# A macaron block on one core: the first phase's tile steps, queued behind the main stream's latest product and lookup

## The chip, the core and the metric

The kernel runs on one core of a Trainium2 chip. The metric is the device time of one execution in microseconds, the median over runs on the chip. The kernel before has 1830.85 us, the median of three runs (1830.73 to 1833.56).

## The reference

The input x has 2 x 2048 tokens of 256 features, 4096 tokens in all. Three residual steps follow one another:

```python
x = x + 0.5 * ffn(layernorm(x), router_w, rg, ru, rd, sg, su, sd)
x = x + attn(layernorm(x), w_qkv, ln_w, w_proj)
x = x + 0.5 * ffn(layernorm(x), router_w, rg, ru, rd, sg, su, sd)
```

The feed-forward part has a shared branch and a routed one. The shared branch sends every token through a gated pair of 256 x 2048 matrices and back: `silu(x @ sg) * (x @ su) @ sd`. The routed branch computes 8 logits of each token, takes the best two experts with weights that add to one, gathers up to 640 tokens for each expert in their order, runs the same kind of gated network with 1024 hidden features, and adds the weighted rows back to their tokens. The attention works in groups of 64 tokens, with 16 heads of 16 features, a causal mask and normalised q and k.

## The kernel before

Matrices are held as pairs of 16-bit numbers, a high part and a low part, and each product of two matrices is computed as three (high by high, high by low, low by high; `TERMS`, L35). The work has four phases, `a` to `d`, in `macaron` (L740 to L821): the first shared branch with its router, the first experts, the attention with most of the second shared branch, and the second experts with the rest.

**The main stream of phase a.** Tokens stand in blocks of 512 (8 blocks), made of four tiles of 128. Phase `a` runs the shared branch for the first four blocks (`NA`). A block goes through 16 chunks of 128 hidden features, so phase `a` has 64 chunks. A chunk is `gate_up` (L326) and `down` (L355). TensorE computes the gate, six matmuls of 512 columns into one PSUM buffer, and then the up part, six more into another (L336; three such buffers go round). ScalarE looks up silu of the gate (L347, "the lookup"). VectorE multiplies it by the up part (L349, "the product"), ScalarE casts the result to its high half hh (L351) and VectorE subtracts to get the low half hl (L352). The twelve matmuls of `down` (L360) read hh and hl; they are traced one chunk later than the product (`defer`, L96). In the first 14 chunks or so VectorE and ScalarE also split the shared weights into pairs (`split`, L101, from `load_shared`, L118).

**The tile steps beside it.** For each of the 32 tiles of all eight blocks, phase `a` also prepares the router and the experts (`tile1`, L766). A tile's steps are: load 128 rows into y (L668, on SyncE's queue); `stats` on VectorE (bn_stats L144, bn_aggr L145, one small operation L147) and a power on GpSimd that gives rstd (L149); the normalised tile z on VectorE (L161); its high half into X on ScalarE (L168) and its low half on VectorE (L169); a transposing DMA from X to xb on SyncE's queue (L178); six small matmuls for the 8 logits (L636), which ScalarE copies out (L223). For tiles of the last four blocks the rows are also copied to `acc` (L772). The first block's four tiles are transposed on TensorE instead (`turn`, L181). After a block's fourth tile comes `route` (L225): max and index, small operations on VectorE and GpSimd, a prefix sum on TensorE, the scatter indices `di` (L284), and then eight scattering DMAs, two for each tile, which GpSimd issues and which read X (`scatter`, L309, L317). X has 16 buffers in this phase, so the copies of a tile wait until the scatters of the tile 16 before it have read theirs. When all are scattered, the first expert's rows are loaded (`expert_load`, L403).

**What sets the order.** Each engine carries out its queue in order. The program is traced by generators: `drive` (L720) advances the main stream and, at a set rate, `Tiles.steps` (L685), which starts a tile every two slots and advances each live tile by one step. A scheduler then orders each engine's queue by a simulated time and the order of tracing, and adds the waits. So where the scheduler believes that a tile's input is early, its step is put ahead of the main stream's next operation, and if the input is late, the operation behind it waits too. An instruction can be tied down: within `self.tc.issue_after(ins)` every instruction that is traced for the engine of `ins` is put somewhere behind `ins` in that queue. `behind` (L191) does so for the instructions in `self.latest`: entry 0 is the latest lookup on ScalarE (set at L347), entry 1 the latest product on VectorE (set at L349); `turn` sets both first (L188). Before the change `behind` is used for the weight splits (L134) and for the first block's copies into X (L653), and for nothing else.

Of the kernel before, what the change touches and what calls it, by code (L numbers as in the profile page):

```python
# [37 lines left out]
class Net:  # L38
    def __init__(self, ctx, tc):
        self.tc = tc  # L40
        self.nc = nc = tc.nc
        pool = lambda name, bufs, **k: ctx.enter_context(tc.tile_pool(name=name, bufs=bufs, **k))
        self.cst = pool("cst", 1)
        self.wsh = pool("wsh", 1)
        self.tok = pool("tok", YB)
        self.xb = pool("xb", NB)
        self.xe = pool("xe", 2)
        self.sm = pool("sm", 2)
        self.dr = pool("dr", 1, space=DRAM)
        self.ps_gu = pool("ps_gu", 3, space=PSUM)  # L50
        self.pend = None
        self.anchor = None
        c = self.cst
        self.tri = c.tile([P, P], BF16, name="tri")
        nc.gpsimd.memset(self.tri, 1.0)
        nc.gpsimd.affine_select(
            out=self.tri, in_=self.tri, pattern=[[1, P]], compare_op=ALU.is_gt,
            fill=0.0, base=0, channel_multiplier=-1)
        self.ones = c.tile([P, P], BF16, name="ones")
        nc.gpsimd.memset(self.ones, 1.0)  # L60
        self.iota8 = c.tile([P, E], F32, name="iota8")
        for e in range(E):
            nc.gpsimd.memset(self.iota8[:, e:e + 1], float(e))
        self.mhalf = c.tile([P, 8], F32, name="mhalf")
        nc.gpsimd.memset(self.mhalf, -0.5)
        self.mone = c.tile([P, 4], F32, name="mone")
        nc.gpsimd.memset(self.mone, -1.0)
        self.e1 = c.tile([P, 4], F32, name="e1")
        nc.gpsimd.memset(self.e1, 2.718281828459045)
        warm = c.tile([P, 8], F32, name="warm")  # L70
        nc.scalar.activation(warm, self.mhalf, AF.Silu)
        tk = self.sm.tile([P, 32], I32, name="tk", bufs=1)
        nc.gpsimd.iota(tk, pattern=[[P, 32]], base=0, channel_multiplier=1)
        self.tokid = c.tile([P, 32], F32, name="tokid")
        nc.vector.tensor_copy(self.tokid, tk)
# [596 lines left out]
class Tiles:  # L672


    def __init__(self, make, count, gap):
        self.make, self.count, self.gap = make, count, gap
        self.slot = 0
        self.live = []
        self.extra = []
        self.nxt = 0  # L680

    def done(self):
# [2 lines left out]
    def steps(self):  # L685

        if self.slot == self.nxt * self.gap and self.nxt < self.count:
            self.live.append(self.make(self.nxt))
            self.nxt += 1
        for g in list(self.extra):  # L690
            r = next(g, "end")
            if r == "end":
                self.extra.remove(g)
            elif r != "stall":
                yield
        for g in list(self.live):
            r = next(g, "end")
            if r == "end":
                self.live.remove(g)
            elif r == "stall":  # L700
                return
            yield
        self.slot += 1


def fed(main, weights):

    for i, _ in enumerate(main):
        if i % 6 == 0:
            next(weights, None)  # L710
        yield


def run_slots(tiles, until):
    while not until():
        for _ in tiles.steps():
            pass


def drive(main, tiles, rate):  # L720

    credit = 0.0
    side = iter(())
    for _ in main:
        credit += 1.0
        for _ in range(2):
            if next(side, "end") == "end":
                break
        if credit >= rate:
            for _ in side:  # L730
                pass
            credit -= rate
            if not tiles.done():
                side = tiles.steps()
    for _ in side:
        pass


@with_exitstack
def macaron(ctx, tc, x, w_qkv, ln_w, w_proj, router_w, rg, ru, rd, sg, su, sd, out):  # L740
    nc = tc.nc
    x = x.rearrange("b s h -> (b s) h")
    out = out.rearrange("b s h -> (b s) h")
    n = Net(ctx, tc)
    R1 = n.route_init(0)
    R2 = n.route_init(1)
    R2["acc"] = out
    x2 = n.dr.tile([T, H], F32, name="x2")
    fbs = {}
    used = set()  # L750
    first = {}, {}

    def new_fb(h, b):
        def get(t):
            if t == 0:
                assert h == 1 or (1, b) in used
                fb = fbs[(h, b)] = n.front_new()
                fb["pe"] = h == 1 and b < PEB
            return fbs[(h, b)]
        return get  # L760

    def tail(R, h, b, t):
        if t == 3:
            yield from n.route(R, b, fbs[(h, b)])

    def tile1(j):  # L766
        b, t = divmod(j, 4)
        y = n.load_tile(x, b, t)
        yield
        yield  # L770
        if b >= NA:
            nc.sync.dma_start(out=R1["acc"][j * P:(j + 1) * P], in_=y)  # L772
        yield from n.front_steps(y, t, new_fb(1, b))
        yield from tail(R1, 1, b, t)
        if j == 31:
            yield from n.expert_load(R1, 0, first[0])

    def tile2(j):
        b, t = divmod(j, 4)
        yield from n.attn_tile(R1, j, x2 if b < NC else out, new_fb(2, b))  # L780
        yield from tail(R2, 2, b, t)
        if j == 31:
            yield from n.expert_load(R2, 0, first[1])

    def ready(h, b):
        return lambda: (h, b) in fbs and fbs[(h, b)]["n"] == 4

    def all_shared(key, b, src, dst, **k):
        yield from n.shared(b, fbs[key]["xb"], src, dst, **k)
        used.add(key)  # L790

    with n.phase("a", BT, 2, 16):
        n.ident = n.at.tile([P, P], F32, name="ident")
        make_identity(nc, n.ident)
        weights = n.load_shared(sg, su, sd)
        next(weights)
        n.load_router(router_w)
        tiles = Tiles(tile1, 32, GAP_A)
        run_slots(tiles, ready(1, 0))
        next(weights)  # L800
        for b in range(NA):
            run_slots(tiles, ready(1, b))
            main = all_shared((1, b), b, x, R1["acc"])
            drive(fed(main, weights) if b == 0 else main, tiles, RATE_A)
        run_slots(tiles, tiles.done)
    with n.phase("b", CAP, 3):
        n.experts(R1, rg, ru, rd, first[0])
    with n.phase("c", BT, 2, 6, SLC):
        n.attn_init(w_qkv, ln_w, w_proj)
        tiles = Tiles(tile2, 32, GAP_C)  # L810
        for b in range(NA, NB):
            drive(all_shared((1, b), b, R1["acc"], R1["acc"], tanh=True), tiles, RATE_C)
        for b in range(NC):
            run_slots(tiles, ready(2, b))
            drive(all_shared((2, b), b, x2, R2["acc"], tanh=True), tiles, RATE_C)
        run_slots(tiles, tiles.done)
    with n.phase("d", CAP, 3):
        n.experts(R2, rg, ru, rd, first[1])
        for b in range(NC, NB):
            for _ in all_shared((2, b), b, out, out, late=10):  # L820
                pass  # L821
# [5 lines left out]
GAP_A = 2  # L827
# [34 lines left out]
```

## Time and profile before

| | |
|---|---|
| median of three runs | 1830.85 us |
| the profiled execution, its own time | 1834.82 us |
| its span in the profile | 1833.1 us |
| mean granted TensorE clock | 0.998 |
| VectorE, 0 to 50 us / 50 to 100 us / 150 to 200 us | 40.82 / 36.05 / 24.89 us busy |
| TensorE, 50 to 100 us / 100 to 150 us / 150 to 200 us | 41.35 / 46.19 / 50.00 us busy |
| first phase's last chunk, product starts | 290.65 us |
| scatters of the first phase | 64, from 56.0 to 256.2 us, mean 1041 ns on GpSimd |

The profile's page gives the busy time of every engine, then tenths of busy time in 40 slices of 45.8 us. The table by stage gives busy us of each engine in a stretch, the number of its instructions, the mean granted clock of TensorE and the DMA share. A line of the waits reads: the engine and line that waited, what it waited for, us in all, how often, and the longest. A line of a timeline gives start, duration, engine, source line and operation, tiles and shapes, and in brackets how long the engine sat idle before it and who ended that. In a timeline the durations of one engine can overlap a little, so the pace is read from the starts.

### The profile page before, as it was taken

The numbers are of one execution on the slowest core, as the hardware profiler recorded it, in microseconds if no ns is written. First come the engines' busy times: TensorE is split into PE (matmuls) and PEld (weight loads), VectorE is DVE, ScalarE is ACT, GpSimd is POOL, SyncE is SP. The second block draws the span as 40 slices with busy tenths as digits, with TensorE's granted clock in tenths as the row PEclk, the third lists the DMA queues.
The fourth block names the chain that finished last, engine by engine and source line by source line (L and its number), as shares of the span: only waits on it lengthen the run. The fifth ranks groups of instructions, "written<-read, shape, count | busy, mean of one in ns | idle before, by whom it ended". The sixth has DMA issues, their size and how long they took to land.

```text
span 1833.1 us, 37526 instructions
## 1 busy us (share of the span) xinstructions
PE 1779.5 (97%) x13724; PEld 1197.0 (65%) x13724; DVE 1199.9 (65%) x2891; ACT 952.9 (52%) x2055; POOL 751.3 (41%) x1072
## 2 busy tenths in 40 slices
PE   7899999999999899999999999999999999999998
PEld 4555556777777556666666666665655677777765
DVE  7754445666666567878777878787656566666643
ACT  5433234555555366666666666666323455555542
POOL 6755530112211334567767676776430011112210
PEclk9999999999999999999999999999999999999999
DMA  7532042455543346668576776766213044455420
GB/s 219 146 90 77 3 88 54 107 118 124 118 113 90 73 77 112 122 118 146 113 146 124 133 142 117 144 101 126 52 27 80 28 111 111 107 120 122 102 47 12
DMA packets 439194, 185.96 MB, mean 101 GB/s; under 512 B 302305, under 2 KB 436125, under 8 KB 439008
## 3 DMA queue, kind: packets, MB, share of 16 engines
q1 hardware_dynamic: 420528, 161.60, 40.7%
q0 software_dynamic: 17664, 21.17, 6.5%
q8 instruction: 107, 1.75, 0.4%
q10 hardware_dynamic: 816, 0.79, 0.1%
q14 instruction: 79, 0.65, 0.1%
HBM read 78.95 MB, written 42.21 MB: 66 GB/s over the span
## 4 chain that ended last, share of the span: by engine, by line
PE 36%; issue 32%; POOL 12%; DVE 10%; DMA 5%; ACT 4%; SPq 0%; POOLq 0%; another core or an unknown queue 0%; DVEq 0%; ACTq 0%
PE pgu L336 22%; PE po L360 11%; POOL xg L317 3%; DVE sl L349 2%; DMA acc<-eo,eidscatter 2%; DVE sl L344 1%; DVE hl L352 1%; POOL X L315 1%; POOL rstd L149 1%; POOL acc L459 1%; ACT hh L351 1%; PE pqk L636 1%; POOL S L583 1%; DVE st L144 1%; POOL e L594 1%
## 5 line engine op out<-in xcount | busy, mean ns | idle before, releaser
L336 PE MATMUL pgu<-xb,sgu 128*128 128x512 f16 x3072 | 742.4, 380 | 18.1 <-DVE sl L349 7.7
L351 ACT CAST hh<-sl 128x512 f16<-128x512 f32 (+2 forms) x512 | 272.8, 533 | 482.9 <-DVE sl L349 466.6
L336 PE MATMUL pgu<-xe,wc 128*128 128x384 f16 (+1 forms) x3072 | 497.0, 299 | 0.0
L336 PEld LDWEIGHTS <-sgu 128*128 128x128 f16 x3072 | 293.4, 98 | 292.9 <-issue 25.8
L349 DVE SCALAR_TENSOR_TENSOR sl<-pgu,sl 128x512 f32<-128x512 f32 (+2 forms) x512 | 300.2, 587 | 227.3 <-PE pgu L336 193.4
L352 DVE TENSOR_TENSOR hl<-sl,hh 128x512 f16<-128x512 f32 (+2 forms) x512 | 311.2, 608 | 161.5 <-ACT hh L351 155.1
L360 PEld LDWEIGHTS <-hh 128*128 128x128 f16 x3328 | 320.3, 98 | 112.3 <-ACT hh L351 7.9
L336 PEld LDWEIGHTS <-wc 128*128 128x128 f16 x3072 | 300.5, 98 | 92.0
L360 PE MATMUL po<-sdw,hh 128*128 128x256 f16 x2048 | 350.1, 273 | 8.1 <-issue 2.8
L360 PE MATMUL po<-sdw,hl 128*128 128x256 f16 x1024 | 247.1, 273 | 14.3 <-DVE hl L352 13.4
L360 PE MATMUL po<-wd,hh 128*128 128x256 f16 x1280 | 223.6, 273 | 0.0
L459 POOL DMA_INDIRECT out_dram<-eo,eidscatter x40 | 65.1, 1627 | 342.1 <-DVE eo L458 332.3
L360 PEld LDWEIGHTS <-hl 128*128 128x128 f16 x1664 | 162.8, 98 | 58.6 <-DVE hl L352 24.2
L347 ACT ACTIVATE sl<-pgu 128x384 f32<-128x384 f32 (+1 forms) x336 | 158.9, 473 | 71.1 <-PE pgu L336 35.5
L459 POOL DMA_INDIRECT acc<-eo,eidscatter x40 | 65.7, 1643 | 296.5 <-DVE eo L458 286.8
L317 POOL DMA_INDIRECT xg<-X,di x128 | 132.3, 1034 | 70.4 <-issue 27.5
L360 PE MATMUL po<-wd,hl 128*128 128x256 f16 x640 | 152.5, 273 | 1.1 <-DVE hl L352 1.1
L344 DVE SCALAR_TENSOR_TENSOR sl<-sl,pgu 128x512 f32<-128x512 f32 x176 | 119.9, 681 | 48.1 <-ACT sl L343 46.1
L343 ACT ACTIVATE sl<-pgu 128x512 f32<-128x512 f32 x176 | 104.2, 593 | 45.3 <-PE pgu L336 39.7
L104 ACT ACTIVATE wc<-re 128x512 f16<-128x512 f32 x128 | 80.5, 629 | 67.9 <-PE pgu L336 57.6
L105 DVE SCALAR_TENSOR_TENSOR wc<-re,wc 128x512 f16<-128x512 f32 x128 | 88.3, 690 | 22.9 <-ACT wc L104 22.6
L583 POOL TENSOR_TENSOR S<-S,amx 128x1024 f32<-128x1024 f32 x32 | 62.0, 1938 | 79.0 <-DVE amx L582 72.1
(150 smaller groups left out, 1713.3 us busy)
## 6 DMA issues: line engine op xcount, KB each, us to landing
re<-in_L_ffn_rg_dram SPq DMA_DIRECT2D x128, 128.0 KB
re<-in_L_ffn_ru_dram SPq DMA_DIRECT2D x128, 128.0 KB
re<-in_L_ffn_rd_dram SPq DMA_DIRECT2D x128, 128.0 KB
y<-acc SPq DMA_DIRECT2D x64, 128.0 KB
y<-in_L_attn_x_dram SPq DMA_DIRECT2D x32, 128.0 KB
acc<-xr SPq DMA_DIRECT2D x16, 256.0 KB
out_dram<-xr SPq DMA_DIRECT2D x16, 256.0 KB
x<-y SPq DMA_DIRECT2D x28, 128.0 KB
```

What stands on the lines that cost most here:

```text
L104: nc.scalar.mul(hi, src, WS)
L105: nc.vector.scalar_tensor_tensor(out=lo, in0=src, scalar=WS, in1=hi, op0=ALU.mult, op1=ALU.subtract)
L317: i = nc.gpsimd.indirect_dma_start(out=R["xg"][:, :], out_offset=bass.IndirectOffsetOnAxis(ap=di[:, t, k:k + 1], axis=0), in_=X, in_offset ...
L336: nc.tensor.matmul(p, lhsT=wc[:, w, i, k, :], rhs=x[:, 2 * a + k, :], start=(j == 0), stop=(j == 5))
L343: nc.scalar.activation(s, p, AF.Tanh, scale=0.5 / XP)
L344: nc.vector.scalar_tensor_tensor(out=s, in0=s, scalar=1.0, in1=p, op0=ALU.add, op1=ALU.mult)
L347: self.latest[0] = nc.scalar.activation(s, p, AF.Silu, scale=1.0 / XP).ins
L349: self.latest[1] = nc.vector.scalar_tensor_tensor(out=s, in0=ps[1], scalar=1.0 / XP / (2.0 * XP if tanh else 1.0), in1=s, op0=ALU.mult, op ...
L351: nc.scalar.copy(h[0], s)
L352: nc.vector.tensor_tensor(out=h[1], in0=s, in1=h[0], op=ALU.subtract)
L360: nc.tensor.matmul(o, lhsT=h[a][:, t * P:(t + 1) * P], rhs=wd[:, w], start=(c == 0 and j == 0 and t % 2 == 0), stop=(c == nch - 1 and j == 2),
L459: i = nc.gpsimd.indirect_dma_start(out=R["acc"][:, :], out_offset=bass.IndirectOffsetOnAxis(ap=ids[:, t:t + 1], axis=0), in_=eo, in_offset ...
```

## The change

Every call that advances a tile in phase `a` is wrapped in `behind` with both entries, once there is a `latest`. So each instruction that a tile step traces for ScalarE is queued behind the latest lookup that has been traced by then, and each that it traces for VectorE behind the latest product. That covers the statistics, z, the copies into X, the copies of the logits and the small operations of `route`. Instructions for TensorE, GpSimd and SyncE get no such tie. The tiles of the attention phase are made without the new argument and are advanced as before. The list `extra`, to which nothing is ever added, is taken out with its loop. The same instructions are issued as before.

```diff
@@ class Net, __init__
         self.pend = None
+        self.latest = None
         self.anchor = None
@@ class Tiles
-    def __init__(self, make, count, gap):
+    def __init__(self, make, count, gap, held=None):
         self.make, self.count, self.gap = make, count, gap
+        self.held = held
         self.slot = 0
         self.live = []
-        self.extra = []
         self.nxt = 0
@@ def steps(self)
-        for g in list(self.extra):
-            r = next(g, "end")
-            if r == "end":
-                self.extra.remove(g)
-            elif r != "stall":
-                yield
         for g in list(self.live):
-            r = next(g, "end")
+            with self.held.behind(self.held.latest is not None, 0, 1) if self.held else nullcontext():
+                r = next(g, "end")
             if r == "end":
                 self.live.remove(g)
@@ def macaron
-        tiles = Tiles(tile1, 32, GAP_A)
+        tiles = Tiles(tile1, 32, GAP_A, n)
```

## The prediction

> **What bounds the kernel now.** The page first: it says which engine is full, and where it is not.
> ```profile
> PE 1779.5 (97%) x13724; PEld 1197.0 (65%) x13724; DVE 1199.9 (65%) x2891; ACT 952.9 (52%) x2055; POOL 751.3 (41%) x1072
> ...
> PE   7899999999999899999999999999999999999998
> ```
> TensorE is the bound: 9 in nearly every slice, except the first two, which lie in the first phase. Only there can an edit of the first phase win anything. The table by stage shows it in us:
> ```profile
> core 0: us, PE busy (x) PEld busy (x) DVE busy (x) ACT busy (x) POOL busy (x), PEclk, DMA share, GB/s
> 20.00:150.00 130.00, 115.97 (x793) 69.04 (x791) 89.19 (x302) 53.27 (x118) 89.39 (x183) 0.99 0.47 126
> 150.00:220.00 70.00, 70.00 (x495) 42.69 (x493) 34.57 (x106) 22.63 (x45) 38.88 (x87) 1.00 0.10 32
> 220.00:292.00 72.00, 66.76 (x419) 39.33 (x418) 31.46 (x92) 21.76 (x40) 18.99 (x34) 1.00 0.30 57
> ```
> TensorE idles 14.0 us between 20 and 150 us, nothing from 150 to 220, and 5.2 us at the end of the phase. The progress of the 64 chunks is read from VectorE's timeline, where each chunk has one product (L349). These are the 2nd, 32nd, 48th and 64th:
> ```profile
> 19.90 0.68 DVE L349 SCALAR_TENSOR_TENSOR sl<-pgu,sl 128x512 f32<-128x512 f32 x1
> ...
> 156.94 0.69 DVE L349 SCALAR_TENSOR_TENSOR sl<-pgu,sl 128x512 f32<-128x512 f32 x1 [0.68 <-PE pgu L336]
> ...
> 221.15 0.69 DVE L349 SCALAR_TENSOR_TENSOR sl<-pgu,sl 128x512 f32<-128x512 f32 x1 [1.99 <-PE pgu L336]
> ...
> 290.65 0.69 DVE L349 SCALAR_TENSOR_TENSOR sl<-pgu,sl 128x512 f32<-128x512 f32 x1 [1.83 <-PE pgu L336]
> ```
> From 32 to 48, TensorE never idle: 64.21/16 = 4.01 us a chunk. From 2 to 32: 137.04 us, where 30 x 4.01 = 120.4 would do, so **16.6 us** are lost. From 48 to 64: 69.50 instead of 64.21, 5.3 us lost. Who causes the loss is in the waits of VectorE and ScalarE from 17 to 150 us:
> ```profile
> DVE z L161 <- POOL rstd L149: 10.7, 6, 4.0
> DVE X L169 <- DMA xg<-X,di: 9.5, 5, 3.1
> DVE X L169 <- ACT X L168: 7.2, 5, 2.7
> ...
> ACT X L168 <- DMA xg<-X,di: 23.3, 10, 3.8
> ```
> These are tile steps that stand ahead of the main stream and wait: the normalised tile z for GpSimd's rstd, the copies into X for a buffer that an earlier scatter still reads. One such place, VectorE and then TensorE:
> ```profile
> 112.46 0.43 DVE L169 TENSOR_TENSOR X<-z,X 128x256 f16<-128x256 f32 x1 [3.08 <-DMA xg<-X,di]
> 112.81 0.68 DVE L349 SCALAR_TENSOR_TENSOR sl<-pgu,sl 128x512 f32<-128x512 f32 x1
> ```
> ```profile
> 113.55 0.59 PE L336 MATMUL pgu<-xb,sgu 128*128 128x512 f16 x2 [2.39 <-DVE sl L349]
> ```
> A side copy waits 3.08 us for a scatter, the product of the main stream is queued behind it, and TensorE idles 2.39 us for the PSUM buffer which that product frees.
>
> **What the change does to the queues.** No instruction is added; each that a tile step issues on VectorE or ScalarE, the route's included, gets an ordering edge behind the latest product or lookup. I counted products ahead of each tile step in the two built programs. Before, 29 of 32 bn_stats stand ahead of the 18th product and all X copies ahead of the 30th. After, a tile comes every 1.7 products: X copies of tiles 4, 8, 16, 24, 31 at 4, 9, 23, 36, 48 (before: 2, 4, 11, 20, 29). Logits keep their places on TensorE from tile 13 on, and the last block's scatter indices (L284) stay at product 53. On SP the row loads, transposes and copies to acc (L668, L178, L772) spread out likewise; the shared-weight loads move ahead of some row loads. The split of those weights stays at products 1 to 12. Removing the list `extra`, which nothing fills, costs nothing.
>
> **What goes.** A 16-deep X pool means that tile j needs the scatter of tile j-16. Before, tile 16 wants its buffer at product 11, when block 0's scatters are just running (56 to 67 us). After, it wants it at product 23, and those scatters start near product 6. So the 23.3 and 9.5 us go, with the 7.2 us behind them. The bunching goes too. Most that can come back is the 16.6 us: 14.0 us of idling, the rest mainly clock, weighed next.
>
> [...]
> ```profile
> 114.00:116.00 2.00, 1.94 (x10) 1.26 (x10) 1.79 (x6) 1.00 (x4) 0.08 (x1) 0.52 0.33 66
> 116.00:118.00 2.00, 2.00 (x10) 1.01 (x9) 0.84 (x2) 0.62 (x1) 0.00 (x0) 0.63 0.33 66
> ```
> Clock 0.52 and 0.63 for 2 us each lose 2 x 0.48 + 2 x 0.37 = 1.7 us. [...]
>
> **What it costs.** (a) *z behind the scatters.* GpSimd is not held back, so rstd now stands behind a block's eight scatters, and its z soon follows on VectorE. A scatter comes every 1.28 us (0.97 busy, 0.30 issue), eight take 10.3; with the column copy and rstd (0.25 + 0.6) rstd is ready 11.2 us after the indices. z stands two products later plus 0.7: 8.7 us. VectorE waits 2.5 us, for blocks 0 to 5: 15 us in all. Queued behind it is the low half hl (L352), and on ScalarE X and the next lookup. hl normally ends 2.1 us after its product; TensorE reads it at the earliest one chunk plus four matmuls later, 4.0 + 0.44. That slack of 2.3 us covers nearly all; each wait leaks 0 to 0.5 us, together 0 to 3: take 1.5. Uncovered it would be 15.
>
> [...]
>
> (b) *VectorE while weights are split* (first 14 chunks). At the measured pace (0.60 from one large instruction to the next, 0.33 for a 256-wide one): main 1.2, splits 3 x 0.60 / 2 = 0.9, tile (4 x 0.33 less one, plus small ones: 1.15) / 1.7 = 0.7, route about 0.45: 3.25 us of 4.01. Free below; above, the pace of the crowded products 2 to 9 before, (50.15 - 19.90)/7 = 4.32, over 14 chunks 4.3 us. Nearer to free, since only this rate remains of the crowd: take 2.
>
> (c) *Logits wait for late transposes.* X to logits was many chunks; it is now 1.7 to 2.5, that is from X's end 4 to 7 us. The same transpose in the attention phase lands 2.41 us after its issue (chain of waits, xt<-xa), so it fits; SP holds row loads ahead of it. 0 to 3 us; take 0.6.
>
> (d) *The end of the phase.* The last scatter indices, scatters, tag and expert weights follow in the same order; the 5.3 us stay, give or take 1.
>
> **Sum.** 16.6 - 1.5 - 2 - 0.6 = 12.5 us. Everything from the experts on keeps its order and TensorE stays its bound, so this carries to the end. The profiled execution took 1834.82 us (span 1833.1, 1.7 around it) and would take 1822.3. It lies 4.0 above the median of the three runs; the same loss taken off 1830.85 gives **1818.4**.
>
> **Rivals.** Likeliest, 0.60: as above, between 1830.85 - 17.3 (all covered, first product 0.7 earlier) = 1813.5 and 1830.85 - 6.3 (each cost at its upper end) = 1824.5. *Half*, 0.20: only the buffer waits go, not those for rstd. Of VectorE's three rows (27.4 us) the buffers hold 9.5 + 7.2, 61%: 10.1 of the 16.6, less 4.1: 6.0, so 1824.9. For it: the trip over GpSimd stays; against: z now has a product between. *It moves the stalls and no more*, 0.08: (a) uncovered takes 15, with the 2.6 of (b) and (c) 1832; the order speaks against it, as the waits come one per block. *Slower*, 0.12: the scatters run slower than 1.28 us, [...]and rstd is late by eight times that. Slower by over 0.2% (3.7 us) needs 16.6 + 3.7 - 2.6 = 17.7 us from six blocks, 3 us each beyond the 2.3 of slack, a VectorE wait of 5.3: 1.6 us a scatter. At 1.8 us: wait 6.7, 4.4 x 6 = 26.4 us lost, 1843. Against: of the 48 scatters before 200 us only 5 ran over 1.3 us.
>
> **Numbers.** 0.2% is about what a measurement of this kernel can tell from no change. Faster 0.80, same 0.08, slower 0.12. The range runs from the best end, 1813.5, into the half case with its scatter, 1828.
>
> **What would show it.** Right: products 2 to 32 in about 124 us; X waiting for no scatter; z waiting for rstd some six times by 2 to 3 us; TensorE idle under 5 us from 20 to 150; the clock never near 0.5; the stretch after product 48 unchanged. Wrong: a VectorE row with waits over 5 us for rstd, TensorE idle before logits, or ScalarE's weight splits late so that TensorE waits for them.

## The result, and the profile after

The changed kernel takes 1828.36 us, the median of 11 runs (1825.66 to 1830.49). The kernel before, run 11 times beside it, has 1833.15 (1830.73 to 1837.23). The ratio is 0.9971 (95% interval 0.9962 to 0.9980): faster, by 3.7 to 7.0 us. The forecast was 12.5 us. The profiled spans are 1833.1 and 1826.6 us, 6.5 apart.

TensorE still sets the end. Its row of the page, and its tenths of busy time in 40 slices:

```profile
PE 1778.0 (97%) x13724; PEld 1197.1 (66%) x13724; DVE 1198.9 (66%) x2891; ACT 951.6 (52%) x2055; POOL 754.5 (41%) x1072
...
PE   6999999999999899999999999999999999999998
```

Two digits of the last line changed: the first slice fell from 7 to 6, the second rose from 8 to 9. Something was won in the first phase and something was lost at its very start. The table by stage for the same three stretches as before (us, then busy us of PE, PEld, DVE, ACT, POOL; clock, DMA share, GB/s; PEld is TensorE loading weights):

```profile
20.00:150.00 130.00, 123.94 (x847) 73.12 (x846) 84.80 (x272) 54.80 (x123) 81.62 (x164) 0.99 0.38 111
150.00:220.00 70.00, 69.59 (x493) 42.27 (x492) 43.18 (x159) 24.78 (x55) 46.24 (x105) 0.99 0.30 73
220.00:292.00 72.00, 70.29 (x453) 43.16 (x451) 35.26 (x107) 23.69 (x44) 22.13 (x38) 1.00 0.31 65
```

TensorE's idle time fell from 14.0 to 6.1 us in the first stretch and from 5.2 to 1.7 in the last. The products of the main stream (now L350), again the 2nd, 32nd, 48th and 64th, from VectorE's timeline:

```profile
25.88 0.68 DVE L350 SCALAR_TENSOR_TENSOR sl<-pgu,sl 128x512 f32<-128x512 f32 x1
...
154.53 0.69 DVE L350 SCALAR_TENSOR_TENSOR sl<-pgu,sl 128x512 f32<-128x512 f32 x1 [1.68 <-PE pgu L337]
...
219.42 0.69 DVE L350 SCALAR_TENSOR_TENSOR sl<-pgu,sl 128x512 f32<-128x512 f32 x1 [1.86 <-PE pgu L337]
...
284.46 0.69 DVE L350 SCALAR_TENSOR_TENSOR sl<-pgu,sl 128x512 f32<-128x512 f32 x1 [0.25 <-PE pgu L337]
```

| product | before, us | after, us | difference |
|---|---|---|---|
| 1st | 16.59 | 22.86 | +6.27 |
| 2nd | 19.90 | 25.88 | +5.98 |
| 2nd to 32nd | 137.04 | 128.65 | -8.39 |
| 32nd to 48th | 64.21 | 64.89 | +0.68 |
| 48th to 64th | 69.50 | 65.04 | -4.46 |
| 64th | 290.65 | 284.46 | -6.19 |

The last difference stays up to the end. So three things happened: the stream starts 6 us late, wins 8.4 us up to product 32, and wins 4.5 us at the end of the phase.

**The late start.** VectorE's timeline of the first 26 us, the changed kernel:

```profile
4.01 0.43 DVE L145 BATCH_NORM_STATS2 st<-y 128x6 f32<-128x256 f32 x1 [1.75 <-DMA y<-in_L_attn_x_dram]
...
7.14 0.42 DVE L188 TENSOR_TENSOR xb<-ptx,xb 128x256 f16<-128x256 f32 x1 [1.19 <-ACT xb L187]
7.48 0.42 DVE L145 BATCH_NORM_STATS2 st<-y 128x6 f32<-128x256 f32 x1
...
10.58 0.42 DVE L188 TENSOR_TENSOR xb<-ptx,xb 128x256 f16<-128x256 f32 x1 [1.19 <-ACT xb L187]
10.92 0.42 DVE L145 BATCH_NORM_STATS2 st<-y 128x6 f32<-128x256 f32 x1
...
17.56 0.42 DVE L188 TENSOR_TENSOR xb<-ptx,xb 128x256 f16<-128x256 f32 x1 [1.25 <-ACT xb L187]
```

And before:

```profile
4.21 0.43 DVE L144 BATCH_NORM_STATS2 st<-y 128x6 f32<-128x256 f32 x1 [1.95 <-DMA y<-in_L_attn_x_dram]
5.40 0.43 DVE L144 BATCH_NORM_STATS2 st<-y 128x6 f32<-128x256 f32 x1 [0.36 <-DMA y<-in_L_attn_x_dram]
6.35 0.77 DVE L144 BATCH_NORM_STATS2 st<-y 128x6 f32<-128x256 f32 x2
...
11.23 0.39 DVE L187 TENSOR_TENSOR xb<-ptx,xb 128x256 f16<-128x256 f32 x1
```

Before, the statistics of four tiles follow within 2.5 us and the last tile is turned at 11.23. After, a tile's statistics start only when the tile before it is turned, one tile every 3.5 us, and the last is turned at 17.56. TensorE's timeline says the same from its side:

```profile
9.45 0.69 PE L186 MATMUL ptx<-ident,z 128*128 128x128 f32 x2 [2.74 <-DVE z L162]
12.97 0.66 PE L186 MATMUL ptx<-ident,z 128*128 128x128 f32 x2 [2.83 <-DVE z L162]
16.45 0.66 PE L186 MATMUL ptx<-ident,z 128*128 128x128 f32 x2 [2.82 <-DVE z L162]
...
17.57 1.86 PE L337 MATMUL pgu<-xb,sgu 128*128 128x512 f16 x4 [0.16 <-ACT xb L187]
```

The reason is in `turn`: it sets `latest` to its own cast and subtraction (L187 and L188), before any main product exists. From then on the new wrapper ties the next tile's steps behind them.

**The middle.** The waits from 17 to 150 us (engine and line, what it waited for, us, times, longest):

```profile
DVE z L162 <- POOL rstd L150: 9.9, 6, 3.8
...
PE pl L637 <- DMA xb<-X: 3.3, 4, 2.1
...
PE pgu L337 <- DVE sl L350: 2.5, 2, 1.5
```

No copy of VectorE or ScalarE into X waits for a scatter any more. Six waits for rstd are left, the number forecast, but of 0.4 to 3.8 us each. And there is a new wait: TensorE waits 3.3 us ahead of logits for transposed tiles. Its longest is the row

```profile
147.83 0.32 PE L637 MATMUL pl<-rwt,xb 128*128 128x8 f16 x6 [2.07 <-DMA xb<-X]
```

after which the table in steps of 2 us shows the granted clock (third number from the end) at 0.95, 0.50 and 0.70:

```profile
146.00:148.00 2.00, 0.17 (x6) 0.17 (x7) 0.46 (x1) 0.23 (x1) 0.99 (x2) 0.95 0.12 7
148.00:150.00 2.00, 2.00 (x13) 0.99 (x11) 0.44 (x1) 0.17 (x1) 0.00 (x0) 0.50 0.69 192
150.00:152.00 2.00, 2.00 (x13) 1.35 (x12) 2.00 (x17) 1.00 (x2) 0.40 (x1) 0.70 0.11 20
```

That is another 2 x (0.05 + 0.50 + 0.30) = 1.7 us.

Two rows of this trace have no cause in it: ScalarE's lookup at 85.19 us and VectorE's product at 141.58 start after 4.60 and 4.91 us of idling whose end the trace gives to no engine of the core ("remote"). Behind the first, TensorE waits 1.46 us at 88.80.

### The profile page after: what moved, and what is told of

It is laid out like the page before. It is cut to its first block, busy times and chain, and to the rows that moved or that the text cites. A ratio compares the mean times of both kernels' runs of the same rounds, so it can differ in the third digit from the quotient of the medians.

```text
span 1826.6 us, 37514 instructions
## 1 busy us (share of the span) xinstructions
PE 1778.0 (97%) x13724; PEld 1197.1 (66%) x13724; DVE 1198.9 (66%) x2891; ACT 951.6 (52%) x2055; POOL 754.5 (41%) x1072
## 4 chain that ended last, share of the span: by engine, by line
PE 47%; issue 21%; POOL 12%; DVE 10%; DMA 5%; ACT 3%; SPq 1%; another core or an unknown queue 1%; POOLq 0%; DVEq 0%; ACTq 0%
PE pgu L337 29%; PE po L361 15%; POOL xg L318 3%; DVE sl L350 2%; DMA acc<-eo,eidscatter 2%; DVE sl L345 1%; DVE hl L353 1%; POOL X L316 1%; POOL rstd L150 1%; POOL acc L460 1%; PE pqk L637 1%; POOL S L584 1%; POOL xa L170 1%; ACT sl L344 1%
## 5 line engine op out<-in xcount | busy, mean ns | idle before, releaser
L350 DVE SCALAR_TENSOR_TENSOR sl<-pgu,sl 128x512 f32<-128x512 f32 (+2 forms) x512 | 300.7, 588 | 244.8 <-PE pgu L337 213.3
```

What stands on the lines that cost most here:

```text
L350: self.latest[1] = nc.vector.scalar_tensor_tensor(out=s, in0=ps[1], scalar=1.0 / XP / (2.0 * XP if tanh else 1.0), in1=s, op0=ALU.mult, op ...
```

## The experiments

Theory A: the missing 6 us are the late start. Rival B: the stream's own waits ate the gain, and a late start is only exchanged for waits that come in any case. Further runs take the forecast's other steps apart. Each time is a median beside runs of the kernel before on the same chip; a ratio has its 95% interval. The runs were made in several sets, so across sets it is the distance to the kernel before that compares. "2 to 32" and "48 to 64" are times between those products in the one profiled execution.

How far can one execution be trusted? From the first product to about the 47th, VectorE and ScalarE carry out the same order in the changed kernel, e1 and e6, but for a few records, and products 2 to 32 take 128.65, 125.38 and 127.88 us. A clock drop of 1.7 us, which e1 lacks, is part of that. So where waits are left, a difference of up to 3 us between two stretches proves little by itself.

| run | us | before, us | ratio | 1st product | 2 to 32 | 48 to 64 | 64th product |
|---|---|---|---|---|---|---|---|
| before | | | | 16.59 | 137.04 | 69.50 | 290.65 |
| after | 1828.36 | 1833.15 | 0.9971 (0.9962 to 0.9980) | 22.86 | 128.65 | 65.04 | 284.46 |
| e1, ties after first product | 1819.64 | 1833.27 | 0.9921 (0.9907 to 0.9934) | 16.14 | 125.38 | 66.12 | 275.74 |
| e2, ties only before it | 1836.28 | 1833.27 | 1.0018 (1.0009 to 1.0026) | 23.65 | 133.13 | 68.40 | 292.74 |
| e6, e1 up to product 48 | 1821.69 | 1833.27 | 0.9932 (0.9918 to 0.9946) | 16.55 | 127.88 | 67.36 | 278.94 |
| e3, before, 32 X buffers | 1829.27 | 1833.27 | 0.9976 (0.9965 to 0.9986) | 17.61 | 132.09 | 67.83 | 285.07 |
| e4, e1, z later | 1812.32 | 1832.99 | 0.9887 (0.9872 to 0.9903) | 16.35 | 119.49 | 67.90 | 270.76 |
| e5, e1, logits later | 1816.11 | 1832.99 | 0.9908 (0.9893 to 0.9923) | 16.82 | 122.40 | 65.44 | 271.11 |
| e7, e1, VectorE only | 1821.06 | 1832.99 | 0.9937 (0.9924 to 0.9951) | 16.76 | 126.86 | 65.55 | 277.26 |
| e8, e1, ScalarE only | 1823.72 | 1832.99 | 0.9954 (0.9941 to 0.9968) | 17.29 | 129.56 | 68.25 | 279.83 |
| e9, e4, tags tied | 1808.01 | 1831.64 | 0.9871 (0.9855 to 0.9886) | 15.86 | 119.48 | 64.64 | 267.00 |
| e10, e9, splits tied | 1806.77 | 1831.64 | 0.9865 (0.9850 to 0.9880) | 16.63 | 119.49 | 63.13 | 266.27 |
| e11, after, z later | 1818.87 | 1831.64 | 0.9932 (0.9919 to 0.9946) | 23.19 | 119.48 | 65.31 | 275.00 |
| e12, before, z later | 1828.84 | 1831.64 | 0.9985 (0.9978 to 0.9992) | 17.41 | 137.21 | 66.82 | 287.61 |

**The start: e1 and e2.** `products` counts the main products traced so far; e1 ties tile steps only when there is one, e2 only while there is none.

```diff
 # e1
-self.held.behind(self.held.latest is not None, 0, 1)
+self.held.behind(self.held.products > 0, 0, 1)
 # e2
-self.held.behind(self.held.latest is not None, 0, 1)
+self.held.behind(self.held.latest is not None and self.held.products == 0, 0, 1)
```

> The tile steps are tied only once the first main product has been traced; the first block's four tiles are prepared as in the kernel before. Theory A (the missing 6.3 us are the late start: the tie to the first block's own transposes puts its tiles one after the other): the first product starts at 16.6 us again instead of 22.9, products 2 to 32 take 127 to 130 us as in the changed kernel, the phase's last product starts near 278, and the time is about 1822, 6 us below the changed kernel. Theory B (the stream's own waits ate the gain, and a later start is only exchanged for waits on weights and tile data that come later in any case): the first product starts early, products 2 to 32 stretch to about 135 us, and the time stays at 1828.

> The other half alone: tile steps are tied while only the first block's transposes exist, and not once a main product exists. Theory A: the first product starts at 22.9 us, the rest runs as in the kernel before, and the time is about 6 us above the kernel before, 1837 to 1839. Theory B: the late start is taken up by the waits that the stream has anyway; products 2 to 32 shorten from 137 to about 131 us and the time is within 1 us of the kernel before.

e1 brings the first product back to 16.14 us and saves 8.7 us against the changed kernel (1828.36 to 1819.64), so A holds, and B does not for this kernel. It is more than the 6 us that A expected: 6.72 us lie ahead of the first product, and the stream behind it, in the same order, is 3.3 us shorter up to product 32, 1.7 of it the clock drop; the rest has no cause on record, and 1.3 us are lost again behind product 32. e1 is 13.6 us below the kernel before; the forecast, which had no late start, was 12.5. e2 has the late start alone and is slower than the kernel before, but by 3.0 us and not by 6: of 7.06 us at the first product 2.09 are left at the 64th, since products 2 to 32 shorten by 3.9. My number for e2 was too high; the kernel before makes up part of a delay, which is what B said of it. In the changed kernel nothing is made up: against e1 it is 6.72 us late at the first product and 8.72 at the 64th.

**The buffers of X: e3.** The pool in phase `a` has 32 buffers in place of 16.

```diff
-with n.phase("a", BT, 2, 16):
+with n.phase("a", BT, 2, 32):
```

> The kernel before with 32 buffers for X instead of 16, so that no copy into X waits for a scatter. It prices the buffer waits alone (VectorE 9.5 us and ScalarE 23.3 us of waits for xg<-X,di). If they and what is queued behind them hold most of the 16.6 us lost between products 2 and 32 (the forecast's half case has 10.1 of them), that stretch falls from 137 to about 127 us and the time by 8 to 10 us. If the waits for rstd are what counts, and take over when the buffers are free, the stretch stays above 133 us and the time falls by less than 4 us. The end of the phase stays at 69 to 70 us from product 48 to 64 either way.

No copy waits for a scatter there, and products 2 to 32 shorten by 4.95 us. That lies between the two cases. Waits for rstd grow from 10.7 to 13.5 us on VectorE (longest 4.5), and TensorE's longest stop, 3.98 us ahead of hl at 74.93 us, comes behind a z that waited 4.46 us for rstd at 71.23. So the buffers are a third of the recoverable time, not the 61% that the forecast's half case counted from VectorE's wait rows; what is queued behind rstd takes over.

**Where z and the logits stand: e4 and e5.** In `front_steps`, e4 waits two more steps between statistics and z, e5 two more between the transposing transfer and the logits; both on top of e1.

```diff
 # e4, behind stats
         yield
+        if keep is None and not fb["pe"]:
+            yield
+            yield
 # e5, behind flip
             yield
             yield
+            if keep is None:
+                yield
+                yield
```

> As the kernel that ties tile steps only after the first product (1819.6 us), with z traced two steps, about one product, later than the statistics, so that rstd is ready when VectorE comes to z. In that kernel VectorE waits 19.9 us for rstd between 17 and 150 us. Theory A (those waits lie in the slack of hl, as forecast, and leak at most 1.5 us): the waits fall below 8 us, products 2 to 32 stay within 1.5 us of 125.4 and the time stays within 1.5 us of 1819.6. Rival (they leak into TensorE's idling of 4.5 us between 50 and 150 us): TensorE's idle falls by 2 us or more and the time to 1817 or less.

> As the kernel that ties tile steps only after the first product (1819.6 us), with the logits traced two steps later, so that the transposing transfer has landed when TensorE comes to them. There TensorE waits 0.49, 0.49 and 1.77 us for xb ahead of logits between 50 and 150 us; in the changed kernel 0.5, 0.5, 0.2 and 2.07 us, the last followed by a drop of the clock. If the late transfers are the largest part of what is still lost there, these rows vanish, products 2 to 32 take 123 us or less, and the time falls to about 1817. If the later logits only push the route and the scatters, and with them waits elsewhere, products 2 to 32 stay at 125 us, or the end of the phase (48 to 64) gets longer by what is won.

e4 refuted my theory on z. Its waits for rstd shrink to

```profile
DVE z L163 <- POOL rstd L151: 3.8, 2, 2.3
```

from 19.9 us in e1, and TensorE is full from 20 to 150 us:

```profile
20.00:150.00 130.00, 129.90 (x914) 79.36 (x912) 91.41 (x306) 57.01 (x122) 87.39 (x187) 1.00 0.40 112
```

The time falls by 7.3 us against e1, products 2 to 32 by 5.9. e5 takes away only the waits ahead of logits, as expected, and wins 3.0 us in that stretch (expected 123 or less, measured 122.40). Why does e4 remove those waits too? (Its edit moves all that follows z in a tile's steps by as much, so it does not part z from the rest.) One place in e1 shows it, on VectorE, SyncE's queue and TensorE in turn:

```profile
134.11 0.93 DVE L163 TENSOR_SCALAR z<-y,mv,rstd 128x256 f32<-128x256 f32 x2 [2.82 <-POOL rstd L151]
```

```profile
136.01 2.83 SPq L180 DMA_TRANSPOSE xb<-X  x2
```

```profile
139.41 0.30 PE L639 MATMUL pl<-rwt,xb 128*128 128x8 f16 x6 [1.77 <-DMA xb<-X]
```

The z of two tiles waits for rstd behind a block's scatters; both go to X together, both transposes stand together on SyncE's queue, and the logits that were placed for an earlier transposed tile stop TensorE. The late rstd is paid on TensorE, by way of X and the transfer. In the changed kernel VectorE does not wait at this pair of z, since the product ahead of it is late itself. But the rstd of both are as late, behind eight scatters (GpSimd, then VectorE):

```profile
140.63 0.97 POOL L318 DMA_INDIRECT xg<-X,di  x1 [0.30 <-issue]
141.60 1.13 POOL L150 TENSOR_TENSOR rstd<-ve,mhalf 128x1 f32<-128x1 f32 x2
```

```profile
141.58 0.69 DVE L350 SCALAR_TENSOR_TENSOR sl<-pgu,sl 128x512 f32<-128x512 f32 x1 [4.91 <-remote]
142.25 0.93 DVE L162 TENSOR_SCALAR z<-y,mv,rstd 128x256 f32<-128x256 f32 x2
```

The two transposes start at 144.14 us and take 3.84 us on SyncE's queue, where one alone takes 1.20, and then comes the wait at 147.83. In e11 (below) two rstd come just as late, at 143.16 us. But their z stand apart, at 143.78 and 146.90, and so do the transposes, at 145.16 and 149.77, and TensorE waits for neither.

**Which tie counts: e7 and e8.** On top of e1, ties for one engine only.

```diff
 # e7
-self.held.behind(self.held.products > 0, 0, 1)
+self.held.behind(self.held.products > 0, 1)
 # e8
-self.held.behind(self.held.products > 0, 0, 1)
+self.held.behind(self.held.products > 0, 0)
```

> Ties after the first product, for VectorE alone: ScalarE's copies of X and of the logits are placed as in the kernel before. If the gain of 13.6 us comes from VectorE no longer standing at z and X ahead of the product, nearly all of it stays: products 2 to 32 in 125 to 128 us, time 1819 to 1823. If ScalarE's queue (23.3 us of waits for the scatters' buffers ahead of the lookup) counts as much, half is lost: products 2 to 32 above 130 us, time about 1826.

> Ties after the first product, for ScalarE alone: z, statistics and the route stay early on VectorE, and the low half of X stays early there too while its high half on ScalarE is late, so VectorE can wait for ScalarE. If VectorE's place in the queue is what counts, little of the gain is left or it is slower than before: products 2 to 32 above 134 us, time 1830 to 1838. If either tie is enough because a tile's steps form one chain over both engines, 127 to 130 us and 1821 to 1825.

VectorE's tie alone keeps 11.9 of the 13.6 us. ScalarE's alone gives 9.3, more than I expected, and without the waits of X for ScalarE that I named; there VectorE's waits are those of early statistics for their rows (27.6 us). The gains do not add up. This fits a tile's steps as one chain over both engines, which spreads when it is held at either end; it was not tested further.

**The late start with z later, and z later alone: e11 and e12.** The edit of e4, on the changed kernel and on the kernel before.

> The changed kernel as it is, with its late start, and z traced two steps later. Theory A (two separate losses, the start and z behind rstd): the first product stays at 22.9 us, products 2 to 32 go from 128.7 to about 120 us with no idle TensorE ahead of logits and no drop of the clock, and the time is the 1812.3 us of the same kernel with the early start plus 6 to 7: 1818 to 1820. Rival (a late start and a late z take the same loss away only once): the time stays above 1824.

> The kernel before with z traced two steps later and no ties. If the ties are what keeps z, X and the rest out of the product's way (the scheduler puts an untied z as early as it believes rstd is there, wherever it was traced), little changes: products 2 to 32 within 3 us of 137, time 1830 to 1835. If tracing z later is enough by itself, that stretch falls below 128 us and the time to about 1824 or less.

e11 has the late start and a stream without waits, 119.48 us, the same as e4: start and z are separate losses. Against e4 the late start costs 6.84 us at the first product and 4.24 at the 64th. The profiled execution of e4 was its slowest, with a clock drop (0.50 from 254 to 256 us); the medians are 6.6 us apart, and 7.9 when each is set against its own runs of the kernel before. e12 leaves the stream at 137.21 us, and z still waits 12.1 us for rstd there (10.7 in the kernel before). That is what was expected if, without the ties, the scheduler places z where it believes rstd to be. It is 2.8 us below the kernel before, a little under my range, all of it behind product 32.

**The end of the phase: e6, e9 and e10.** e6 ends e1's ties at product 48. e9 ties an expert's four tag operations (L417 to L421) behind the latest product, on top of e4. e10 also ties the first expert's first three weight splits behind products 61, 62 and 63 (`marks` keeps each product and its lookup).

```diff
 # e6
+self.held.behind(0 < self.held.products < 48, 0, 1)
 # e9, in expert_load
+        with self.behind(True, 1):
             nc.vector.tensor_tensor(out=tk, in0=tag[:, :, 0].bitcast(I32), in1=R["bits"][:, e], op=ALU.bitwise_and)
...
 # e10, in experts
+        with self.after_mark(60 + c if R["key"] == "scatter0" and e == 0 and c < 3 else None):
             self.split(wc[:, 0], wc[:, 1], r)
             self.split(wd[:, 0], wd[:, 1], r2)
```

> As the first kernel of this call, but the ties end with product 48. It tells where the 4.5 us between products 48 and 64 come from. If the order of the last tile steps gives them (steps of tiles 28 to 31 and of the first expert load behind the products), the stretch from 48 to 64 goes back to about 69 us from 65, and the time is 4 to 5 us above the first kernel of this call. If they come from the tiles being evenly spread earlier, so that the last tiles are no longer late or early, the stretch stays at 65 us and the times agree within 1 us.

> As the kernel with the ties after the first product and z two steps later (1812.3 us, products 48 to 64 in 67.9 us where 64.2 would do), with the small VectorE operations on an expert's tags tied behind the product that is the latest when they are traced, so that those of experts 1 to 7 no longer stand ahead of product 64. If they hold the end of the phase up (VectorE waits 4.2 us for tags there, TensorE then 1.0 us for sl), the stretch shortens by 1 to 2 us, and the first products of the experts come another 1 us earlier; time about 1810. If the wait of ScalarE for the first expert's weights (7.2 and 2.2 us, TensorE 1.97 us idle and the clock after it) is all that counts, less than 1 us is won.

> As the kernel with the tied tag operations of this call, and the splits of the first expert's first three weight chunks tied behind the products 61, 62 and 63 (before, the first two stood near products 59 and 60 and waited for their loads ahead of the main stream's casts). If that wait is what lengthens the end of the phase, products 48 to 64 take 64 to 65 us, TensorE does not idle there and its clock stays at 1.0; time 3 us below the tied tags alone, about 1807. If the loads are late for the experts as well, the wait goes to the first expert's matmuls, and the time stays within 1 us of the tied tags alone.

In the traces the tag operations of all eight experts start behind products 56 to 60 in the kernel before and in e6; in the changed kernel and in e1 two start behind 57 and the others behind 61 and 62. e6's stretch is 67.36 us against e1's 66.12, and the medians are 2.0 us apart with intervals that overlap: less than the 4 to 5 us expected of the order, and not clear of nothing. In e9 the stretch is 3.3 us shorter than in e4 (67.90 to 64.64), above the 1 to 2 expected. But 2.5 us of that are not the tags': ahead of hh TensorE waits 1.97 us in e4 and 1.21 in e9, and only in e4 does a clock drop follow (0.95, 0.50 and 0.70 from 252 to 258 us, which makes 1.7 us). That leaves 0.8 us for the tags, and 1.02 more behind product 64 (TensorE's wait at 277.83 us in e4, which e9 does not have). Set against their own runs of the kernel before, the medians are 3.0 us apart, and the intervals overlap. The wait ahead of hh comes from a weight split on ScalarE, here in e4:

```profile
252.13 0.63 ACT L106 ACTIVATE wc<-re 128x512 f16<-128x512 f32 x1 [7.23 <-DMA re<-in_L_ffn_ru_dram]
```

```profile
253.33 0.62 PE L363 MATMUL po<-sdw,hh 128*128 128x256 f16 x4 [1.97 <-ACT hh L354]
```

ScalarE stood 7.23 us at the split, the cast to hh was queued behind it, and TensorE waited for that. With the splits further back, in e10, TensorE is full to the end of the phase:

```profile
220.00:292.00 72.00, 72.00 (x496) 47.86 (x495) 36.12 (x92) 29.12 (x57) 13.24 (x28) 1.00 0.30 69
```

The stretch falls by another 1.5 us. By the medians e10 is only 1.2 us below e9, and their intervals overlap, so the 3 us expected were not there. e10 beats both kernels: at 1806.77 us it is 24.9 below the kernel before, where the changed kernel is 4.8 below.

## Why the prediction was wrong

The direction was right, and so was the main mechanism in the middle: the copies into X no longer wait for scatters ahead of the product. The size was wrong, mostly by two terms: one that the sum did not have, the start, and one priced far too low, late z and logits.

**The start, missing in the sum.** The prediction followed the products from the 2nd to the 64th and let the first start no later (its range even allowed 0.7 us earlier). The tie holds from the first `turn`, not from the first product, and the four tiles that everything waits for became a serial chain of 3.5 us each. It costs 5.98 us at product 2 against the kernel before; taking it away (e1) brings 6.72 us at the first product and 8.7 in all. The code said so (L187 to L189), and the order shows it: the statistics of tile 1 stand behind the turn of tile 0. I counted products ahead of each tile step, and for the first block there were none to count.

**What can come back.** Forecast 16.6 us between products 2 and 32, measured 137.04 - 119.48 = 17.6 (e11), at 3.98 us a chunk where 4.01 was taken. Right.

**(a) z behind the scatters, and (c) the logits.** The waits on VectorE came to the sum forecast, 9.9 us up to 150 us and 15.3 in the whole phase, where 15 was forecast; in part this is luck. Only two of the ten, 3.73 us at 53.75 and 4.05 at 172.36, are for an rstd behind a block's scatters. The largest of the others, 3.77 us at 71.88, is for one behind the route's small operations and column copies on GpSimd (63.74 to 71.27), which the forecast did not count.

The failed assumption is where a late rstd is paid. I set the waits against the slack of hl and took 1.5 us, and priced late transposes by themselves at 0.6. In the changed kernel TensorE waits 1.00 us (at 75.08) for a PSUM buffer that a product behind such a z frees, and 3.3 us ahead of logits, with 1.7 of clock behind it: 6.0 of the 9.2 us that its stretch is longer than e11's. I cannot assign the other 3.2 to z; 1.46 of them are the wait behind the lookup without a cause. e11 shows that all 9.2 go when z and the steps behind it come later, and e4 that 5.9 go on top of e1: (c) is largely (a) seen from TensorE. Forecast together 2.1, measured 9.2. "TensorE idle before logits" was among the forecast's own signs of being wrong, and it came.

**(b) VectorE beside the weight splits.** Forecast 2 us; e11 has the same splits and TensorE is full from 20 to 100 us (80.00 us busy). Measured 0.

**(d) The end of the phase.** Forecast unchanged within 1 us, measured 4.46 us shorter. "In the same order" was wrong: nearly all tags moved from products 56 to 60 to products 61 and 62. e9 and e10 show that tags and splits make this stretch long, the splits more. How much of the 4.46 is their order alone stays open: e6, with the old order, is 1.2 us longer than e1, and 2.1 us shorter than the kernel before, each in one execution.

**The sum.** -12.5, +5.98 for the start, +4.1 in the middle, +0.7 from 32 to 48 and -4.5 at the end is -6.2, the trace's difference. The last term is luck: nothing in the forecast foresaw it, and without it the gain in the trace would have been 1.7 us. The rivals: the half case gave 1824.9, and the buffers are worth even less than it gave them (e3: 4.95 of 16.6). The slower case needed scatters far above 1.28 us, and none of it was seen: the eight scatters of a block start 1.30 to 1.38 us apart on average, where the case needed 1.6, and the longest wait for rstd in the phase is 4.1 us, where it needed 5.3. Its reason, that each scatter also waits for the one eight back, cost nothing that the traces show: between 17 and 292 us GpSimd waits ahead of a scatter for another's transfer twice in the kernel before, 0.3 us each, as long as its idle time between two scatters of a block, and never in the changed kernel. But the mechanism that nearly decided was none of these three: it sits ahead of the stream.

**The clock.** The forecast counted 1.7 us of clock behind a gap of 2.39 us, from the rows of the kernel before. The changed kernel shows the same: 2.07 us of idling, then a clock of 0.50 and 0.70, again 1.7 us. What could come back, 17.6 us, is also nearer the 16.6 with those 1.7 us than the 14.9 without. The runs add that the length of the gap does not decide alone (last section).

## What to carry to other kernels

When an ordering edge refers to "the latest" operation, ask what that is before the loop has begun: the tiles that fill the pipeline may be tied to each other. And follow a late operand to the engine that sets the end, through every queue on the way (here z, X, a transposing transfer, logits on TensorE); slack at the nearest consumer says nothing of the others. Then give the producer time by where the consumer is placed: two steps between statistics and z were worth more than the whole change.

## What the runs showed of the hardware

The clock drop after idling of about 2 us came in several runs, but not by length alone. Gaps of 1.97 us (e4, at 253 us), 2.07 (after) and 2.52 (e6, at 141 us) were followed by 0.50 and then 0.70 or 0.79. In e2 TensorE idled longer, on its timeline

```profile
61.48 0.28 PE L363 MATMUL po<-sdw,hl 128*128 128x256 f16 x1 [2.66 <-DVE hl L355]
```

and the clock in steps of 2 us stayed at 1.00:

```profile
60.00:62.00 2.00, 0.52 (x5) 0.48 (x6) 2.00 (x5) 0.75 (x2) 1.85 (x6) 1.00 0.50 129
62.00:64.00 2.00, 2.00 (x13) 1.10 (x12) 2.00 (x7) 1.14 (x3) 2.00 (x10) 1.00 0.54 137
```

Seven of these traces have such a drop between 18 and 292 us (the kernel before, the changed kernel, e3, e4, e6, e8 and e12), and each makes 1.7 us in the steps of 2 us. In steps of 0.1 us the clock stands at 0.50 for 3.4 us, from 114.08 to 117.49 us in the kernel before and from 147.78 to 151.20 in the changed kernel. In the 3.4 us ahead of its drop TensorE had idled 1.9 to 3.4 us in all in each of the seven. In e12 these were 1.96 us in pieces, the longest 1.54, while a single gap of 3.39 us in the same run (up to 73.91 us) left the clock at 1.00. Nothing here was made to test what decides between a drop and none, so that stays open.
